# Quarter 0 of a gated projection: a written VectorE order with parts between the sums, last sums of f placed earlier, first output weights summed later

## The chip, the cores and the metric

The kernel runs on one core of one Trainium2 chip, as one launch. The metric is the device time of a launch in microseconds (us). A core has a matrix engine (TensorE, PE in the profile; its weight loads are PEld), a vector engine (VectorE, DVE), a scalar engine (ScalarE, ACT), GpSimd (POOL) and a queue that issues the transfers (SyncE, SP). Each engine takes its instructions in the order in which they stand in its queue, and waits on semaphores for what other engines produce. Matmuls write PSUM banks of 128x512 fp32; DVE, ACT and POOL read and write SBUF, and DVE and ACT read the banks.

## The reference

A graph network with four layers of cross attention and a gated feed-forward block, between two graph convolutions. N = 1024 rows, D = 512, 8 heads, 16 groups of 256 condition rows, L = 4 layers, all in fp32. What this case changes lies in the feed-forward block of each layer:

```python
for i in range(L):
    a = _attn(_ln(h, ln2_w[i], ln2_b[i]), cond, Wq[i], Wk[i], Wv[i], Wo[i])
    h = h + a
    u = _ln(h, ln3_w[i], ln3_b[i]) @ geglu_w[i] + geglu_b[i]      # (1024,512) @ (512,4096)
    val, gate = jnp.split(u, 2, axis=-1)
    f = val * jax.nn.gelu(gate, approximate=False)                 # (1024, 2048)
    h = h + f @ ffo_w[i] + ffo_b[i]                                # (1024,2048) @ (2048,512)
```

## The kernel before

**Seven products.** Large matrix products are done by a Strassen-like scheme: both operands are cut into 2x2 blocks, sums of blocks are formed (on DVE or POOL), seven block products run on PE instead of eight, and sums of the results give the output. Every product is then followed by an addition that reads its bank, and a bank is used for a second product only when that addition has read it.

**The quarters.** The feed-forward block of a layer runs in four quarters r = 0..3, each with 512 columns of val and the matching 512 of gate. Each quarter has four pieces c = 0..3 of 128 columns. A quarter gives f (tiles fT, two halves f0 and f1 per piece), and `ffn_out` multiplies f by 512 rows of the output weights and adds the result onto h.

**Quarter 0 (class `Quad`, L934 to L981).** It works in plain fp32, with four matmuls of 128x512 per product. Products 0 and 1 of each quad go to a bank ga during the end of the attention (`first`, `second`). `rest` then does products 5, 6, 4, 3, 2 into the banks gb, gc, gd, gc, gd. DVE adds: u2 from gb, u3 from gc (L967), g1 from gd (L970), g0 from gc (L974), then v1 (tile gv, L978) from gd, f1 (L980) and f0 (L981). ACT applies Gelu to g1 and g0 (L957). The fifth matmul group of a quad overwrites gd, so it waits for L970; the fourth overwrites gc after L967.

**The right blocks' parts.** The quarters 1 to 3 (class `Chunk`) use matmuls of a faster type for which every operand is split in a high, a low and a middle part. For six of the seven right blocks (ln3T and ln3S, the turned normalised rows and their sums) these parts are made once per layer, during quarter 0: `begin_right` gives the high part on ACT and the middle part gr on DVE in two halves of 128x512 (L1090), `finish_right` the low part gl, one DVE operation of 128x1024 (L1096). In `parts_beside(c)` two blocks are begun behind the last addition of each of the quads 0 to 2, and after quad 2 the low parts of blocks 0 and 1 follow. Blocks 5 and 6 get theirs ahead of the first `ffn_out`, blocks 4 and 3 ahead of the second. No order is written for this stretch: the scheduler sets each engine's order by its own estimates.

**The left parts of a chunk.** For each chunk (r, c) POOL forms sums of the weights (gxa, gy, L1138), ACT scales a high part (gha, ghb, L1103), DVE forms a low part (gla of 128x1024, glb of 128x512, L1104) and POOL their difference (gsa, gsb, L1105). The chunk's matmuls are L1154, its additions L1189 (gu, g), L1172 (a scaled addition in a bank), f0 (L1220) and f1 (L1223). These are pinned: they keep the order in which the program writes them.

**Sums of f and the output product.** `Gated.sums` (L1293 to L1301) forms the sums of f that `ffn_out` needs: for c = 0 and 1 one subtraction (a21), for c = 2 and 3 three operations fs (s2, s1, s4). `ffn_out` (L1330 to L1348) runs twice per quarter, each with seven products of eight matmuls in the order fa, fc, fd, fb, fa, fc, fd. The first fd needs fs. The first fa is read by DVE (`kept`, L1340; in quarter 0 by an ACT copy) before the second fa may overwrite its bank; fc is read by an addition onto hall (L1336) before the second fc. At a quarter boundary (r = 1 to 2, and 2 to 3) the first `ffn_out` of the old quarter stands behind the first chunk of the new one, and DVE has the old quarter's last f1, then this chunk's gu, g and glb, then the three fs, then the next chunk's gla, then `kept`.

**The output weights.** `out_weights` forms four sums on POOL (wffs, L216 to L219). For r = 0 it is written ahead of `geglu` and comes to stand, in POOL's queue, during the last attention group, whose probabilities DVE scales at L804, whose transposes DVE copies at L836 (pT), and for which PE's mixing matmuls po (L822) wait.

Of the kernel before, what the change touches and what calls it, by code (L numbers as in the profile page):

```python
# [25 lines left out]
def gnn_kernel(  # L26
# [26 lines left out]
    nc = tc.nc  # L53
# [9 lines left out]
    KC = D // P  # L63
# [19 lines left out]
    @contextmanager  # L83
    def waiting_for(ins, engine):

        traced = nc.cur_bb.bb.instructions
        n = len(traced)
        yield
        for i in traced[n:]:
            if i.engine == engine:  # L90
                tc.add_manual_dep(i, ins.ins.name, mybir.DependencyInfo(
                    mybir.DependencyClass.Sync, mybir.DependencyReason.DATA))

    def bank(name):
        return psum.tile([P, 512], F32, tag="bank", name=name)

    def t512(name, dtype=F32):
        return work.tile([P, 512], dtype, tag="t512", name=name)

    def slot(name):  # L100
        return slots.tile([P, 2, 512], F32, tag="slot", name=name)

    def slots_of(n, name):
        return [slot(f"{name}_{i}") for i in range(n)]
# [91 lines left out]
    gcols = const.tile([P, L * 2 * DFF // P], F32, name="gcols")  # L196
# [11 lines left out]
    h = [hall[:, nb, :] for nb in range(NB)]  # L208
# [4 lines left out]
    def sums_of_b(t, b11, b12, b21, b22, t1, t2, t4, t_last=None):  # L213


        t.tensor_tensor(t1, b12, b11, OP.subtract)  # L216
        t.tensor_tensor(b12, b22, b12, OP.subtract)
        t.tensor_tensor(t2, b22, t1, OP.subtract)
        return (t_last or t).tensor_tensor(t4, b21, t2, OP.subtract)  # L219
# [8 lines left out]
    def halves_of(t):  # L228
        return t.rearrange("p (a b) -> p a b", a=2)
# [62 lines left out]
    def blocks_of_w(w):  # L292
        return [w[k][:, :, d * M:(d + 1) * M] for d in range(2) for k in range(2)]
# [15 lines left out]
    def of_k(w, right):  # L309
        return lambda i, to, start: multiply(  # L310
            to, w[i], right[i], [(c * P, (c + 1) * P, 0, M) for c in range(2)], start)
# [5 lines left out]
    def begin(l, g, x, of, s1, behind=None):  # L317

        t = slots_of(2, f"{x}_{l}_{g}")
        a = bank(f"pa_{x}_{l}_{g}")  # L320
        of(0, a, True)
        nc.scalar.copy(s1, a)
        of(1, a, False)
        with tc.issue_after(behind.ins) if behind else nullcontext():
            nc.scalar.copy(blocks_out(t)[0], halves_of(a))
        return t, s1
# [51 lines left out]
    high = gp.tile([ET, P], F32, name="high")  # L378
# [17 lines left out]
    pc = bank("pc")  # L396
# [201 lines left out]
    def add_left(left, rows, to, root, name):  # L598

        for d in range(NB):  # L600
            nc.sync.dma_start(left.rearrange("p a b -> p (a b)"), left_dram[d])
            pl = bank(f"left_{name}_{d}")
            for s in range(NB):
# [8 lines left out]
             for step in project_steps(nb, h0T, w_in, "in",  # L612
# [5 lines left out]
    begun = {"k0": begin(0, 0, "kT", of_k(blocks_of_w(raw_wk), conds[0, 0]), firsts[:, 0, :],  # L618
                         shifted_last)}
# [83 lines left out]
    def acc_tile(name):  # L703
        return accs.tile([P, 512], F32, tag="acc", name=name)
# [221 lines left out]
    def out_weights(t, l, r, wff):  # L926
        s = slots_of(2, f"wffs_{l}_{r}")
        b11, b12, b21, b22 = (wff[k][:, :, d * M:(d + 1) * M] for k in range(2) for d in range(2))
        t1, t2, t4 = (halves_of(s[i // 2][:, i % 2, :]) for i in range(3))
        sums_of_b(t, b11, b12, b21, b22, t1, t2, t4)  # L930
        return [b11, b21, b22, t4, t1, t2, b12]

    class Quad:
# [5 lines left out]
            self.cv = l * 2 * DFF // P + r * KC + c  # L939
            self.left, self.right = left, right  # L940

        def product(self, i, to, start):
            multiply(to, self.left[i], self.right[i],
                     [(self.c * P, (self.c + 1) * P, 0, 512)], start)

        def first(self):
            self.a = bank(f"ga_{self.n}")
# [8 lines left out]
            cg = self.cv + DFF // P  # L956
            nc.scalar.activation(pre, pre, AF.Gelu, bias=gcols[:, cg:cg + 1])  # L957

        def rest(self):
            n, c, bias = self.n, self.c, gcols[:, self.cv:self.cv + 1]  # L960
            pb, pc, pd = (bank(f"{x}_{n}") for x in ("gb", "gc", "gd"))
            self.product(5, pb, True)
            u2 = acc_tile(f"gu2_{n}")
            nc.vector.tensor_tensor(u2, pb, self.s1, OP.add)
            self.product(6, pc, True)
            u3 = acc_tile(f"gu3_{n}")
            nc.vector.tensor_tensor(u3, pc, u2, OP.add)  # L967
            self.product(4, pd, True)
            g1 = t512(f"g1_{n}")
            nc.vector.tensor_tensor(g1, pd, u3, OP.add)  # L970
            self.gate(g1, n)
            self.product(3, pc, False)
            g0 = t512(f"g0_{n}")
            nc.vector.tensor_tensor(g0, pc, u2, OP.add)  # L974
            self.gate(g0, n)
            self.product(2, pd, False)
            v1 = acc_tile(f"gv1_{n}")
            nc.vector.scalar_tensor_tensor(v1, pd, bias, u2, OP.add, OP.add)  # L978
            f0, f1 = self.f.of(c)
            nc.vector.tensor_tensor(f1, v1, g1, OP.mult)  # L980
            return lambda: nc.vector.scalar_tensor_tensor(f0, self.a, bias, g0, OP.add, OP.mult)  # L981

    def inner_left(t, x, s1, s2, s4):

# [96 lines left out]

    SPLIT = (0, 5, 6, 4, 1, 3)

    def begin_right(name, x, h, s):

        nc.scalar.mul(h.bitcast(F32R), x, INWARD / TINY)
        for k in range(2):
            more = t512(f"{name}_{k}")
            nc.scalar.mul(more, h[:, k, :], 1.0 + TINY)
            nc.vector.scalar_tensor_tensor(s.bitcast(F32R)[:, k, :], x[:, k, :], 1.0 / TINY, more,  # L1090
                                           OP.mult, OP.subtract)

    def finish_right(name, x, h, s):

        low = slot(name)
        nc.vector.scalar_tensor_tensor(low.bitcast(F32R), x, 1.0 / TINY, h, OP.mult, OP.subtract)  # L1096
        return h, low, s

    pin = tc.keep_in_program_order

    def split_left(x, h, l, s):

# [122 lines left out]
    class KeyPair(InStep):  # L1225
# [3 lines left out]
        x = "k"  # L1229
# [77 lines left out]
    def quads_of(l, r, left, right):  # L1307
        f = Gated(l, r)
        return f, [Quad(l, r, c, left, right, f) for c in range(KC)]

    def geglu(quads, f, beside):
        for c, q in enumerate(quads):
            q.last = q.rest()()
            beside(c)
            f.sums(c)

    def ffn_out(l, r, s, left, right, kept, each=lambda ins: ins):

# [82 lines left out]
    class QueryPair(InStep):  # L1401


        x = "q"
# [134 lines left out]
    for l in range(L):  # L1539

        wk, wv, wq, wo, ffb, spare = projections
        if l:
# [13 lines left out]
            kT_1, _ = keys(l, 1, wk)  # L1556
# [169 lines left out]
        g = NG - 1  # L1726
        kT, v = kTs[g], vs[g]
        f, quads = quads_of(l, 0, left, right)
# [25 lines left out]
        raw_out = load_out(l, 0)  # L1754
        more = [slot(f"gr_{l}_{i}") for i in range(2 * len(SPLIT) - 2)]
        wide = four_wide(f"gr_{l}")
        more.extend(wide[:, 2 * i:2 * i + 2, :] for i in range(2))
        begun = {i: (right[i], *more[2 * n:2 * n + 2]) for n, i in enumerate(SPLIT)}
        Chunk.rights = {2: right[2]}

        def finish_rights(*of):
            for i in of:
                Chunk.rights[i] = finish_right(f"gl_{l}_{i}", *begun[i])

        def parts_beside(c):
            with tc.issue_after(quads[c].last.ins):
                for i in SPLIT[2 * c:2 * c + 2]:
                    begin_right(f"gt_{l}_{i}", *begun[i])
                if c == 2:
                    finish_rights(0, 1)  # L1770

        wff = out_weights(nc.gpsimd, l, 0, raw_out)
        geglu(quads, f, parts_beside)
        chunks = [(r, c) for r in range(1, R) for c in range(KC)]
        ready = []

# [11 lines left out]

        load()
        sum_chunk(0)  # L1790
        finish_rights(5, 6)
        ffn_out(l, 0, 0, f.left(), wff, kept, pin)
        split(0, False)
        split(0, True)
        load()
        sum_chunk(1)
        finish_rights(4, 3)
        ffn_out(l, 0, 1, f.left(), wff, kept, pin)
        split(1, False)
        load()  # L1800
        raw_out = load_out(l, 1)
# [5 lines left out]
        before = None  # L1807
        for r in range(1, R):
            for c in range(KC):
                chunk = ready.pop(0)  # L1810
                flow = chunk.steps(lambda: sum_chunk(1), lambda: split(0, True))
                chunk.f = f if c else Gated(l, r)
                next(flow)
                if c > 2 or r == 1 and c or r > 1 and c == 0:
                    split_next(0)
                for _ in range(3):
                    if before:
                        next(before, None)
                    next(flow)
                if before:  # L1820
                    f.sums((c - 1) % KC, nc.vector, pin)
                before = flow
                if c == 0:
                    kept_f, f = f, chunk.f
                if r > 1 and c < 2:
                    split_next(1)
                    ffn_out(l, r - 1, c, kept_f.left(), wff, kept, pin)
                    if c == 1:
                        raw_out = load_out(l, r)
                if c == (KC - 1 if r + 1 < R else KC - 2):  # L1830
                    wff = out_weights(nc.gpsimd, l, r, raw_out)
# [61 lines left out]
    class Rows:  # L1893
# [12 lines left out]
        def add(self, row, at, of, engine=nc.vector):  # L1906
            at = self.base[row][:, at]
            engine.tensor_tensor(at, of, at, OP.add)  # L1908
# [85 lines left out]
```

## Time and profile before

| what | value |
|---|---|
| time, median of 3 runs | 2483.92 us (2483.9 to 2483.96) |
| the profiled execution's own time | 2488.66 us |
| its span, first to last instruction | 2486.1 us |
| mean granted TensorE clock | 0.990 |
| busy PE, DVE, POOL, ACT | 97%, 68%, 41%, 34% |

In the profile, a row of a timeline gives start and duration in us, engine, source line, operation, output tile and input tiles, shape, count, and in brackets the idle time of the engine before it with what ended it. A row with x4 or x8 is a run of equal instructions. Rows of waits give the waiting tile and line, what it waited for, the total, the number of times and the longest. Matmuls are pipelined, so rows of PE overlap a little: the distance from start to start is the cost. A duration on DVE or POOL counts from when the instruction enters the engine, so it holds time in which it could not yet work.

### The profile page before, as it was taken

The numbers are of one execution on the slowest core, as the hardware profiler recorded it, in microseconds if no ns is written. First come the engines' busy times: TensorE is split into PE (matmuls) and PEld (weight loads), VectorE is DVE, ScalarE is ACT, GpSimd is POOL, SyncE is SP. The second block draws the span as 40 slices with busy tenths as digits, with TensorE's granted clock in tenths as the row PEclk, the third lists the DMA queues.
The fourth block names the chain that finished last, engine by engine and source line by source line (L and its number), as shares of the span: only waits on it lengthen the run. The fifth ranks groups of instructions, "written<-read, shape, count | busy, mean of one in ns | idle before, by whom it ended". The sixth has DMA issues, their size and how long they took to land. (4 is left out here: it accounts for less than half of the span.)

```text
span 2486.1 us, 35090 instructions
## 1 busy us (share of the span) xinstructions
PE 2407.7 (97%) x13032; PEld 1888.3 (76%) x13032; DVE 1696.2 (68%) x3248; ACT 839.6 (34%) x1784; POOL 1012.4 (41%) x1059
## 2 busy tenths in 40 slices
PE   8999999999999999999999999999999999999999
PEld 5678886577787887477787888477787888567787
DVE  9665566877676557776676557777785656777764
ACT  7323333343213334342313324433323333433320
POOL 0433444274453223264453224345544222536531
PEclk9999999999999999999999999999999999999999
DMA  5323220111302220011122211011131031011140
GB/s 178 121 69 113 90 94 18 42 43 51 119 31 77 89 74 18 21 56 43 56 110 68 77 66 47 9 51 51 43 132 68 14 124 52 1 51 35 51 144 35
DMA packets 118064, 163.55 MB, mean 66 GB/s; under 512 B 9256, under 2 KB 66928, under 8 KB 117888
## 3 DMA queue, kind: packets, MB, share of 16 engines
q1 hardware_dynamic: 115792, 155.81, 19.0%
q0 software_dynamic: 1376, 4.30, 0.5%
q8 instruction: 107, 1.75, 0.3%
q10 hardware_dynamic: 720, 1.11, 0.1%
q14 instruction: 69, 0.57, 0.1%
HBM read 138.12 MB, written 23.07 MB: 65 GB/s over the span
## 5 line engine op out<-in xcount | busy, mean ns | idle before, releaser
L1168 ACT ACTIVATE g<-g 128x512 f32<-128x512 f32 x192 | 112.1, 584 | 311.5 <-PE g L1154 307.7
L1105 POOL TENSOR_TENSOR gsa<-gha,gla 128x1024 fp32r<-128x1024 f32 x48 | 115.4, 2404 | 155.0 <-DVE gla L1104 155.0
L1105 POOL TENSOR_TENSOR gsb<-ghb,glb 128x512 fp32r<-128x512 f32 x48 | 79.9, 1664 | 215.4 <-DVE glb L1104 215.4
L799 ACT ACTIVATE pr<-sc,nmax 128x256 f32<-128x256 f32 x256 | 118.2, 472 | 91.6 <-DVE nmax L794 91.1
L1154 PE MATMUL g<-gr,gsa 128*128 128x512 f32 x384 | 136.6, 437 | 0.0
L1330 PE MATMUL fa<-wff,fT 128*128 128x256 f32 x512 | 124.4, 385 | 0.2
L300 PE MATMUL pa_v<-wv,ct 128*128 128x256 f32 x512 | 123.9, 385 | 0.0
L997 POOL TENSOR_TENSOR kr<-ct,ct 128x256 f32<-128x256 f32 x48 | 36.9, 768 | 211.5 <-DVE pr L804 206.9
L1154 PE MATMUL g<-gr,gha 128*128 128x512 f32 x384 | 122.8, 401 | 0.0
L300 PE MATMUL pd_v<-wvs,ct 128*128 128x256 f32 x512 | 121.0, 379 | 0.0
L300 PE MATMUL pc_v<-wv,ct 128*128 128x256 f32 x512 | 121.0, 379 | 0.0
L1154 PE MATMUL g<-gl,gla 128*128 128x512 f32 x384 | 118.6, 390 | 0.0
L1330 PEld LDWEIGHTS fa<-wff,fT 128*128 128x128 f32 x512 | 99.6, 195 | 21.3 <-issue 5.0
L300 PEld LDWEIGHTS pa_v<-wv,ct 128*128 128x128 f32 x512 | 94.9, 190 | 22.5 <-issue 9.2
L794 DVE TENSOR_REDUCE nmax<-sc 128x2 f32<-128x512 f32 x128 | 83.7, 679 | 41.2 <-PE sc L787 41.2
L1181 ACT ACTIVATE g<-g,gcols 128x512 f32<-128x512 f32 x96 | 67.4, 702 | 128.2 <-DVE g L1189 125.0
L300 PEld LDWEIGHTS pd_v<-wvs,ct 128*128 128x128 f32 x512 | 97.3, 190 | 13.2
L300 PEld LDWEIGHTS pc_v<-wv,ct 128*128 128x128 f32 x512 | 97.0, 190 | 13.0
L1330 PE MATMUL fd<-wffs,fs 128*128 128x256 f32 x256 | 71.9, 418 | 34.1 <-DVE fs L1300 34.1
L1154 PEld LDWEIGHTS g<-gr,gsa 128*128 128x128 f32 x384 | 71.9, 188 | 33.4 <-issue 16.3
L804 DVE TENSOR_SCALAR pr<-pr,inv 128x256 f32<-128x256 f32 x256 | 90.4, 396 | 2.9
L1220 DVE SCALAR_TENSOR_TENSOR fT<-g,gcols,g 128x512 f32<-128x512 f32 x48 | 35.9, 749 | 80.1 <-ACT g L1181 79.8
(516 smaller groups left out, 6352.5 us busy)
## 6 DMA issues: line engine op xcount, KB each, us to landing
ct<-cond_dram SPq DMA_DIRECT2D x72, 512.0 KB, 5.6
wff<-in_L_gnn_ffo_w_dram SPq DMA_DIRECT2D x32, 512.0 KB, 4.3
cond_dram<-ct SPq DMA_DIRECT2D x24, 512.0 KB, 3.0
gxb<-in_L_gnn_geglu_w_dram SPq DMA_DIRECT2D x96, 128.0 KB, 2.3
gxa<-in_L_gnn_geglu_w_dram SPq DMA_DIRECT2D x96, 128.0 KB, 2.3
cond<-in_L_gnn_cond_dram SPq DMA_DIRECT2D x32, 256.0 KB, 4.6
ct<-cond_dram SPq DMA_DIRECT2D x24, 256.0 KB, 5.8
wk<-in_L_gnn_Wk_dram SPq DMA_DIRECT2D x8, 512.0 KB, 6.3
```

The lines of the kernel that those rows point to most:

```text
L300: each(nc.tensor.matmul(at, left[:, k, l0:l1], right[:, k, r0:r1], start=start and n == 0 and k == 0, stop=n == len(cols_of) - 1 and k == ...
L794: nc.vector.tensor_reduce(nmax, ps3, AX.X, OP.max, negate=True)
L799: nc.scalar.activation(pr3[:, a, :], ps3[:, a, :], AF.Exp, bias=nmax[:, a:a + 1], accum_out=tot[:, a:a + 1])
L804: scores.last = nc.vector.tensor_scalar(pr3[:, a, :], pr3[:, a, :], inv[:, a:a + 1], None, OP.mult)
L997: t.tensor_tensor(to, of, less, OP.subtract)
L1105: pin(nc.gpsimd.tensor_tensor(s.bitcast(F32R), h, l, OP.subtract))
L1154: pin(nc.tensor.matmul(to, self.part(i, which)[:, k, :], self.rights[i][which].bitcast(F32R)[:, k, :], start=start and k == 0, stop=stop a ...
L1168: pin(nc.scalar.mul(to, to, 1.0 + TINY))
L1181: pin(nc.scalar.activation(to, of, AF.Gelu, bias=gcols[:, cg:cg + 1]))
L1220: pin(nc.vector.scalar_tensor_tensor(f0, a, bias, g0, OP.add, OP.mult))
L1330: each(nc.tensor.matmul(to[:, q * M:(q + 1) * M], left[i][k][:, (2 * s + q) * P:(2 * s + q + 1) * P], right[i][:, k, :], start=start and q ...
```

## The change

Each layer is changed in the same way, in five parts.

1. `Quad.rest` is pinned, on PE and DVE. After u2, u3, g1, g0 and after the end of a quad it calls `fill()`, which issues the next right block's part. v1 is replaced by an addition of u2 onto gd in the bank, f0 comes ahead of f1, and f1 reads the bank.
2. The parts come from a generator, in the order of blocks 0, 1, 5, 6, 4, 3. `finish_right` makes the low part in two halves of 128x512 instead of one operation of 128x1024, and blocks 0 and 1 get theirs right after their middle part.
3. `out_weights` for r = 0 is written after quad 0, and its POOL operations wait for the last addition of quad 0 (`q.last`).
4. In quarter 0 the sums of f of c = 0, 1 and 2 are formed on POOL instead of DVE, those of c = 3 on DVE, pinned.
5. At the boundaries from quarter 1 to 2 and 2 to 3, `f.sums(KC - 1)` of the old quarter is issued right behind its f1, two steps of the new chunk earlier than before.

On DVE the order of quarter 0 becomes, per quad: u2, part, u3, part, g1, part, g0, part, gd += u2, f0, f1, part. The sixteen parts so placed are twelve halves gr and four halves gl (blocks 0 and 1); they are used up in quad 3. Then come the three fs of c = 3, gl of blocks 5 and 6 in halves, and the additions of `ffn_out`. gl of blocks 4 and 3 are four halves behind the gla and glb of chunk (1, 0). PE's order is the same but for gb of the later quads, which is no longer split. SP's order is the same.

```diff
-        def rest(self):
-            n, c, bias = self.n, self.c, gcols[:, self.cv:self.cv + 1]
...
+        def rest(self, fill):
...
+            def add(to, x, y):
+                self.last = pin(nc.vector.tensor_tensor(to, x, y, OP.add))
+
+            self.product(5, b, True, pin)
+            add(u2, b, self.s1)
+            fill()
+            self.product(6, c, True, pin)
+            add(u3, c, u2)
+            fill()
+            self.product(4, d, True, pin)
+            add(g1, d, u3)
             self.gate(g1, n)
+            fill()
+            self.product(3, c, False, pin)
+            add(g0, c, u2)
             self.gate(g0, n)
-            self.product(2, pd, False)
-            v1 = acc_tile(f"gv1_{n}")
-            nc.vector.scalar_tensor_tensor(v1, pd, bias, u2, OP.add, OP.add)
-            f0, f1 = self.f.of(c)
-            nc.vector.tensor_tensor(f1, v1, g1, OP.mult)
-            return lambda: nc.vector.scalar_tensor_tensor(f0, self.a, bias, g0, OP.add, OP.mult)
+            fill()
+            self.product(2, d, False, pin)
+            add(d, d, u2)
+            pin(nc.vector.scalar_tensor_tensor(f0, self.a, bias, g0, OP.add, OP.mult))
+            pin(nc.vector.scalar_tensor_tensor(f1, d, bias, g1, OP.add, OP.mult))
+            fill()
...
-    def finish_right(name, x, h, s):
+    def finish_right(name, x, h):
         low = slot(name)
-        nc.vector.scalar_tensor_tensor(low.bitcast(F32R), x, 1.0 / TINY, h, OP.mult, OP.subtract)
-        return h, low, s
+        for k in range(2):
+            yield low
+            pin(nc.vector.scalar_tensor_tensor(low.bitcast(F32R)[:, k, :], x[:, k, :], 1.0 / TINY,
+                                               h[:, k, :], OP.mult, OP.subtract))
...
-        wff = out_weights(nc.gpsimd, l, 0, raw_out)
-        geglu(quads, f, parts_beside)
+        def all_parts():
+            for i in (0, 1, 5, 6, 4, 3):
+                yield from begin_right(f"gt_{l}_{i}", *begun[i])
+                if i < 2:
+                    yield from finish_rights(i)
+
+        parts = all_parts()
+        next(parts)
+
+        def fill():
+            next(parts, None)
+
+        for c, q in enumerate(quads):
+            q.rest(fill)
+            if c == 0:
+                with waiting_for(q.last, mybir.EngineType.Pool):
+                    wff = out_weights(nc.gpsimd, l, 0, raw_out)
+            f.sums(c, nc.gpsimd if c < 3 else nc.vector, pin)
+        for _ in parts:
+            pass
...
-                for _ in range(3):
+                for step in range(3):
                     if before:
                         next(before, None)
+                        if step == 2 and c == 0:
+                            f.sums(KC - 1, nc.vector, pin)
                     next(flow)
-                if before:
-                    f.sums((c - 1) % KC, nc.vector, pin)
+                if c:
+                    f.sums(c - 1, nc.vector, pin)
                 before = flow
```

More of the change, by code (lines that the diff above doesn't have):

```diff
@@ L940, in __init__, with product @@
             self.left, self.right = left, right
-        def product(self, i, to, start):
+        def product(self, i, to, start, each=lambda ins: ins):
             multiply(to, self.left[i], self.right[i],
-                     [(self.c * P, (self.c + 1) * P, 0, 512)], start)
+                     [(self.c * P, (self.c + 1) * P, 0, 512)], start, each)
         def first(self):
@@ L957, in gate @@
             nc.scalar.activation(pre, pre, AF.Gelu, bias=gcols[:, cg:cg + 1])
-        def rest(self):
-            n, c, bias = self.n, self.c, gcols[:, self.cv:self.cv + 1]
[L961 to L970, printed above, removed]
+        def rest(self, fill):
+            n, bias = self.n, gcols[:, self.cv:self.cv + 1]
+            b, c, d = (bank(f"{x}_{n}") for x in ("gb", "gc", "gd"))
+            u2, u3 = (acc_tile(f"g{x}_{n}") for x in ("u2", "u3"))
+            g0, g1 = (t512(f"{x}_{n}") for x in ("g0", "g1"))
+            f0, f1 = self.f.of(self.c)
+            def add(to, x, y):
[8 more added lines that the diff above has]
+            add(g1, d, u3)
             self.gate(g1, n)
-            self.product(3, pc, False)
-            g0 = t512(f"g0_{n}")
-            nc.vector.tensor_tensor(g0, pc, u2, OP.add)
+            fill()
+            self.product(3, c, False, pin)
+            add(g0, c, u2)
             self.gate(g0, n)
-            self.product(2, pd, False)
-            v1 = acc_tile(f"gv1_{n}")
-            nc.vector.scalar_tensor_tensor(v1, pd, bias, u2, OP.add, OP.add)
-            f0, f1 = self.f.of(c)
-            nc.vector.tensor_tensor(f1, v1, g1, OP.mult)
-            return lambda: nc.vector.scalar_tensor_tensor(f0, self.a, bias, g0, OP.add, OP.mult)
+            fill()
[4 more added lines that the diff above has]
+            fill()
     def inner_left(t, x, s1, s2, s4):
@@ L1082, in gnn_kernel @@
     SPLIT = (0, 5, 6, 4, 1, 3)
+    pin = tc.keep_in_program_order
     def begin_right(name, x, h, s):
@@ L1089, in begin_right @@
             nc.scalar.mul(more, h[:, k, :], 1.0 + TINY)
-            nc.vector.scalar_tensor_tensor(s.bitcast(F32R)[:, k, :], x[:, k, :], 1.0 / TINY, more,
-                                           OP.mult, OP.subtract)
-    def finish_right(name, x, h, s):
+            yield
+            pin(nc.vector.scalar_tensor_tensor(s.bitcast(F32R)[:, k, :], x[:, k, :], 1.0 / TINY,
+                                               more, OP.mult, OP.subtract))
+    def finish_right(name, x, h):
         low = slot(name)
-        nc.vector.scalar_tensor_tensor(low.bitcast(F32R), x, 1.0 / TINY, h, OP.mult, OP.subtract)
-        return h, low, s
-    pin = tc.keep_in_program_order
+        for k in range(2):
+            yield low
+            pin(nc.vector.scalar_tensor_tensor(low.bitcast(F32R)[:, k, :], x[:, k, :], 1.0 / TINY,
+                                               h[:, k, :], OP.mult, OP.subtract))
     def split_left(x, h, l, s):
@@ L1309, in quads_of @@
         return f, [Quad(l, r, c, left, right, f) for c in range(KC)]
[L1311 to L1315, printed above, removed]
     def ffn_out(l, r, s, left, right, kept, each=lambda ins: ins):
@@ L1762, in finish_rights @@
             for i in of:
[L1763 to L1770, printed above, removed]
-        wff = out_weights(nc.gpsimd, l, 0, raw_out)
-        geglu(quads, f, parts_beside)
+                x, high, mid = begun[i]
+                flow = finish_right(f"gl_{l}_{i}", x, high)
+                Chunk.rights[i] = high, next(flow), mid
+                yield
+                for _ in flow:
+                    yield
+        def all_parts():
[15 more added lines that the diff above has]
+            pass
         chunks = [(r, c) for r in range(1, R) for c in range(KC)]
@@ L1790, in gnn_kernel @@
         sum_chunk(0)
-        finish_rights(5, 6)
+        for _ in finish_rights(5, 6):
+            pass
         ffn_out(l, 0, 0, f.left(), wff, kept, pin)
@@ L1796, in gnn_kernel @@
         sum_chunk(1)
-        finish_rights(4, 3)
+        for _ in finish_rights(4, 3):
+            pass
         ffn_out(l, 0, 1, f.left(), wff, kept, pin)
```

## The prediction

> **What bounds the kernel now.** I read the page first, then the waits of the matmul engine, then the timelines around each of those waits.
>
> ```profile
> PE 2407.7 (97%) x13032; PEld 1888.3 (76%) x13032; DVE 1696.2 (68%) x3248; ACT 839.6 (34%) x1784; POOL 1012.4 (41%) x1059
> ```
>
> TensorE (PE) is busy for 97% of the span, and the diff takes no matmul away. So the change is worth what it does to PE's waits and to its clock. The waits of PE, grouped (total us, times, longest):
>
> ```profile
> PE fd L1330 <- DVE fs L1300: 34.1, 15, 3.6
> PE gd L300 <- DVE g L970: 18.2, 4, 5.0
> PE po L822 <- DVE pT L836: 5.8, 4, 1.5
> ```
>
> All three lie in stages that the change touches: quarter 0 (gd, and some of the fd waits), the quarter boundaries (the other fd waits), and the last attention group ahead of quarter 0 (po).
>
> **Quarter 0 as it is.** PE's timeline at the end of quarter 0, in layer 0 and (last two lines) in layer 3, then VectorE's (DVE) in layer 0, and the granted clock there (0.80, the last column but two):
>
> ```profile
> 458.85 1.88 PE L300 MATMUL gc<-ln3S,wgate 128*128 128x512 f32 x4
> 465.68 3.78 PE L300 MATMUL gd<-ln3T,ges 128*128 128x512 f32 x4 [4.95 <-DVE g L970]
> 469.25 3.07 PE L1330 MATMUL fa<-wff,fT 128*128 128x256 f32 x8
> 476.44 1.89 PE L1330 MATMUL fb<-wffs,fs 128*128 128x256 f32 x8
> ```
>
> ```profile
> 2188.78 1.88 PE L300 MATMUL gc<-ln3S,wgate 128*128 128x512 f32 x4
> 2205.61 1.89 PE L1330 MATMUL fb<-wffs,fs 128*128 128x256 f32 x8
> ```
>
> ```profile
> 458.08 1.82 DVE L1090 SCALAR_TENSOR_TENSOR gr<-ln3T,gt 128x512 fp32r<-128x512 f32 x2
> 459.82 2.34 DVE L1090 SCALAR_TENSOR_TENSOR gr<-ln3S,gt 128x512 fp32r<-128x512 f32 x2
> 462.08 2.35 DVE L1096 SCALAR_TENSOR_TENSOR gl<-ln3T,gr 128x1024 fp32r<-128x1024 f32 x2
> 464.95 0.68 DVE L970 TENSOR_TENSOR g<-gd,gu 128x512 f32<-128x512 f32 x1
> ```
>
> ```profile
> 460.00:477.00 17.00, 11.49 (x33) 7.36 (x32) 14.48 (x19) 3.50 (x5) 1.53 (x2) 0.80 0.16 46
> ```
>
> A product starts 1.72 to 1.73 us after the one before it when nothing waits (fa and fc of the boundary fence below, 555.11 and 556.84). From the start of gc to that of fb lie five products, 8.6 us; here it is 17.59, so 8.97 are lost. In layer 3 it is 16.83 (8.2 lost); between them layers 1 and 2 lose 8.45 and 7.86: 33.5 us in all. The cause is DVE's queue: it runs six right-block parts (gr, gl) before g, for whose read of bank gd the next product waits. Of the loss in layer 0 some 5.1 is that gap, 0.56 a wait of fd on fs, and 3.3 the half clock that follows (gd and fa take 3.78 and 3.07 instead of 1.88); over the four layers this tail averages 2.6 (33.5 less the waits, over 4).
>
> **Quarter 0, changed.** With g1 and g0 each ahead of a part, no more than one part stands between two sums. Per quad DVE has seven sums (0.6 each back to back) and four parts. Prices of the parts and of POOL's adds:
>
> ```profile
> 439.86 1.29 DVE L1090 SCALAR_TENSOR_TENSOR gr<-ln3T,gt 128x512 fp32r<-128x512 f32 x2
> 428.26 9.87 POOL L1611 TENSOR_TENSOR hall<-hall,ffb 128x512 f32<-128x512 f32 x8
> ```
>
> That is 7 x 0.6 + 4 x 0.65 = 6.8 us in a quad of 8.6, so DVE fits if it runs alone. It doesn't: four wffs sums, two a21 subtracts and three fs sums now sit on POOL beside it, 9 x 1.23 = 11.1 us, after the hall adds, which quad 0 already meets. Rows below show that a DVE operation with two SBUF inputs and a POOL add run one after the other. Where POOL has a queue, a part then takes about 1.3 instead of 0.65, and a quad of DVE 7 x 0.6 + 4 x 1.3 = 9.4 us, 0.8 more than PE's 8.6. The lag is small in quad 0, shows in quad 1 and is largest in quad 2, until a21 is done; quad 3 meets only fs. Laid out in queue order with these durations, PE waits 0.7 and 0.1 in quad 1, 1.8 in quad 2 and 0.1 in quad 3, 2.7 per layer (0 if POOL never collides; 5.5, twice that, if each part waits for a whole add). None is near the gaps that draw the half clock, so that tail goes, and fd hardly waits for fs: its second sum ends some 0.5 us ahead of fd, so each further 0.5 of lag in quad 3 would come back as that wait. What is late next is gl_4 and gl_3, cut into four halves behind the next chunk's splits:
>
> ```profile
> 485.88 5.58 DVE L1096 SCALAR_TENSOR_TENSOR gl<-ln3S,gr 128x1024 fp32r<-128x1024 f32 x2
> 485.44 2.73 POOL L1105 TENSOR_TENSOR gsa<-gha,gla 128x1024 fp32r<-128x1024 f32 x1 [23.84 <-DVE gla L1104]
> ```
>
> Two wide operations let two POOL operations in (5.58 us); four halves let in four, at about 7.3 us. The add on fc behind them holds PE's second fc, about 1.4 us more per layer. So layer 0 gains 8.97 - 2.7 - 1.4 = 4.9, the others 4.4, 3.8 and 4.1: **-17 us** (-28 without collisions, -6 with 5.5 us of them in each layer).
>
> The rest of quarter 0 costs nothing: the removed gv is replaced by an in-place add of the same length, f1 now reads a bank (0.66 instead of 0.60, covered by the 1.8 us a quad that DVE has spare), ScalarE's copies follow its gates at 34% busy, and no DMA is added or passes another on SP's queue. POOL's queue takes the wffs sums behind quad 0's last add; behind them wait a21, fs and the gxa sums of the next chunk, whose first reader (gsa) stands at 485, over 20 us later. Without that cover it would be 5 us.
>
> **First output weights moved: the po wait.** Timelines of layer 0 before quarter 0:
>
> ```profile
> 402.37 2.18 DVE L804 TENSOR_SCALAR pr<-pr,inv 128x256 f32<-128x256 f32 x2
> 407.28 0.62 DVE L804 TENSOR_SCALAR pr<-pr,inv 128x256 f32<-128x256 f32 x2
> 401.79 1.27 POOL L216 TENSOR_TENSOR wffs<-wff 128x512 f32<-128x512 f32 x1
> 412.94 2.08 PE L822 MATMUL po<-pT,v 128*64 128x64 f32 x62 [1.46 <-DVE pT L836]
> ```
>
> While POOL sums wffs (four such rows, to 407), a pair of scalings takes 2.18 instead of 0.62, and the next pair likewise. That delay, over 1.5 us, stands in DVE's queue ahead of the copies of the transposes for which po waits. With POOL empty there, the 1.46 goes in each layer: **-5.8 us** (0 if another link of that chain is as late).
>
> **Last sums of f at the boundaries.** Where quarter 1 meets 2 and 2 meets 3 (eight places) PE's ffn_out waits for fs. First and last of the eight (first fa, fd, second fa, fc; then first and second fa), then DVE, POOL and ACT:
>
> ```profile
> 542.88 1.89 PE L1330 MATMUL fa<-wff,fT 128*128 128x256 f32 x8
> 550.49 2.93 PE L1330 MATMUL fd<-wffs,fs 128*128 128x256 f32 x6 [3.57 <-DVE fs L1300]
> 555.11 1.89 PE L1330 MATMUL fa<-wff,fT 128*128 128x256 f32 x8
> 556.84 1.89 PE L1330 MATMUL fc<-wffs,fT 128*128 128x256 f32 x8
> ```
>
> ```profile
> 2341.63 1.89 PE L1330 MATMUL fa<-wff,fT 128*128 128x256 f32 x8
> 2353.90 1.89 PE L1330 MATMUL fa<-wff,fT 128*128 128x256 f32 x8
> ```
>
> ```profile
> 543.08 0.74 DVE L1223 SCALAR_TENSOR_TENSOR fT<-g,gcols,g 128x512 f32<-128x512 f32 x1
> 548.10 1.21 DVE L1299 TENSOR_TENSOR fs<-fT,fT 128x512 f32<-128x512 f32 x1
> 549.34 1.10 DVE L1300 TENSOR_TENSOR fs<-fs,fT 128x512 f32<-128x512 f32 x1
> 552.03 1.21 DVE L1104 SCALAR_TENSOR_TENSOR gla<-gha,gxa 128x1024 fp32r<-128x1024 f32 x1
> 553.16 0.68 DVE L1340 TENSOR_TENSOR kept<-fa,kept 128x512 f32<-128x512 f32 x1
> ```
>
> ```profile
> 543.77 2.37 POOL L1105 TENSOR_TENSOR gsa<-gha,gla 128x1024 fp32r<-128x1024 f32 x1
> 546.90 1.85 POOL L1138 TENSOR_TENSOR gxa<-gxa 128x256 f32<-128x256 f32 x2
> 549.85 1.71 POOL L1105 TENSOR_TENSOR gsb<-ghb,glb 128x512 fp32r<-128x512 f32 x1
> ```
>
> ```profile
> 545.71 0.72 ACT L1181 ACTIVATE g<-g,gcols 128x512 f32<-128x512 f32 x1 [4.80 <-DVE g L1189]
> 546.34 0.61 ACT L1103 ACTIVATE ghb<-gxb 128x512 fp32r<-128x512 f32 x1
> 548.79 1.06 ACT L1103 ACTIVATE gha<-gxa 128x1024 fp32r<-128x1024 f32 x1 [1.84 <-POOL gxa L1138]
> ```
>
> Second fa starts 12.23 us after the first (four products are 6.9): 5.33 lost; 5.37 at the last, 43.0 over the eight. Of each, 3.7 is the gap and on average 1.65 the half clock after it. The rows also show the alternation: fs from 548.10 gets going when gxa ends at 548.75; the next fs, 549.34, ends at 550.44, and gsb, recorded from 549.85, ends 1.12 later at 551.56.
>
> Changed, fs stands right behind f1, ready at 543.85. But gsa has begun at 543.77, so the first sum starts at 546.14; then DVE and POOL take turns (0.56 each): the second sum ends at 547.8, the third at 549.0. PE's fd starts near 547.9, 2.6 earlier, its wait down to 1.0. Queued behind fs are now gu, g, glb: g1 ends at 550.8 instead of 545.6. ACT's gate (0.72, then ghb 0.61, then gha 1.06) ends gha at 553.25; glb at 552.2 lets gsb in at 552.85 for 1.12, gla follows at 553.95 for 1.13, and only then kept, to 555.7. Second fa needs kept, for it overwrites the bank that kept reads. It starts at 555.75, 0.6 later than now: fb ends near 550.9, so a gap of 4.85 opens one product later. The half clock's tail then comes after it, not inside: 1.65 by the eight gaps of 3.6, 2.6 by quarter 0's four of 4.4 to 5; I take 2.1, between these. Per boundary: 5.97 + 2.1 - 5.38 = 2.7, **+21.6 us** over eight. Low end +8: the first sum beats gsa (0.55 less), gla beats gsb (0.65 less), tail 1.65. High end +31: tail 3.3, the largest of quarter 0.
>
> **The sum.** -17 - 5.8 + 21.6 = -1.2 us. The profiled execution took 2488.66 us (span 2486.1), 0.2% over the median 2483.92; the sum is laid on the median: 2482.7, say 2483. About 0.2%, 5 us, is what a measurement of this kernel tells from no change.
>
> **The rivals.**
> Kept in time (gain): at the boundaries the low end holds, so second fa loses no more than now plus a little: -22.8 + 8 = -15, 2469 us. For it: f1 and gsa are 0.08 apart, so the order of first arrival could turn. Against: the chain gate, gha, gla, kept is 5 us long whoever wins first.
> Half clock rare (gain): the tail follows only a gap that empties a whole period of 3.41 us; a gap of 4.85 does so in (4.85 - 3.41)/3.41 = 42% of positions, so the tail is 1.1: 5.97 + 1.1 - 5.38 = 1.7, +13.5, sum -9, 2475 us. Against: fd at 2.93 after a wait of 3.57, which can hardly empty one. The Trainium skill, "TensorE: Matmul & The Clock Gate" (Part 1, What's actually happening), gives this rule: half speed after at least one idle window of about 3.4 us on a free-running grid; by it the time would be 2475, and the tails after gaps of 3.57 here speak against it.
> All removed (gain): fs early ends the boundary loss and kept is never late: -43 - 22.8, 2418 us. Against: the queue order above.
> Longer half clock (slower): the gap of 4.85 leaves two periods in a row mostly idle and each boundary pays 3.3 of tail: +31 - 22.8 = +8, 2492 us. It decides from a tail of 2.9 on (+5). For it: layer 0's quarter 0 pays that after 4.95.
> Quarter 0 collides (slower): POOL adds fall on parts in a row and PE waits 5.5 instead of 2.7, -6 instead of -17: +10, 2494 us. For it: the DVE rows 458.08 and 459.82, 1.82 and 2.34 instead of 1.29 beside three small POOL adds. Against: three of four quads have DVE time to spare.
>
> **How the numbers follow.** Forecast (within 0.2%) 0.30; kept in time 0.18, half clock rare 0.12, all removed 0.05: faster 0.35. Longer half clock 0.20, quarter 0 collides 0.15: slower 0.35. Likeliest single case: 2483, by itself 2479 to 2489. The range holds all but "all removed" and the far end of both slower cases at once (2484 + 9 + 11 = 2504): 2462 to 2502.
>
> **What would show it.** PE's gd waits (18.2) nearly gone and replaced by waits below 2 us in quads 1 to 3; po waits gone; at the boundaries a wait of fd on fs near 1 us and a new wait of second fa on kept (L1340's twin) near 4.8, with fa or fc at half clock behind it; fs recorded long, beside gsa. Wrong if kept comes before 554, or if quarter 0 shows gaps above 3 us again.

## The result, and the profile after

The changed kernel takes 2477.41 us (median of 7 runs, 2476.35 to 2477.92) against 2483.98 us (median of 7 runs). The ratio is 0.9965, 95% interval 0.9954 to 0.9977: faster by 0.35%, some 6.6 us by the medians. The forecast was 2483 us, no change; the range of 2462 to 2502 holds the result, and it belongs to the 0.35 that stood on faster. The runs of the kernel before lie in two groups, near 2484 and near 2488; its profiled execution is one of the upper group, so the two profiles differ by more than the medians, 10.5 us in span.

The page of the changed kernel and its grouped waits of TensorE (total us, times, longest):

```profile
span 2475.6 us, 35108 instructions
PE 2401.2 (97%) x13032; PEld 1883.8 (76%) x13032; DVE 1701.2 (69%) x3252; ACT 837.2 (34%) x1784; POOL 1050.7 (42%) x1079
```

```profile
PE fa L1333 <- DVE kept L1343: 37.8, 8, 4.7
PE fd L1333 <- DVE fs L1309: 8.7, 11, 0.9
PE fc L1333 <- DVE hall L1339: 4.7, 4, 1.2
...
PE gc L300 <- DVE gu L967: 3.2, 4, 0.8
```

The waits of gd (18.2) and po (5.8) are gone. Of the 34.1 us of fd on fs 8.7 are left, but in their place stands a new row, second fa on kept: 37.8 us in eight places, one per boundary.

The same instruction in both timelines tells where the time went. In layer 0, the kernel before (first ga after po, first matmul of chunk (1, 0), first matmul after the first boundary's output product):

```profile
414.95 1.12 PE L300 MATMUL ga<-ln3T,wval 128*128 128x512 f32 x2
...
495.49 0.81 PE L1154 MATMUL g<-gr,gha 128*128 128x512 f32 x2
...
560.10 0.81 PE L1154 MATMUL g<-gr,gha 128*128 128x512 f32 x2
```

and the changed kernel:

```profile
412.89 1.12 PE L300 MATMUL ga<-ln3T,wval 128*128 128x512 f32 x2
...
486.92 0.82 PE L1163 MATMUL g<-gr,gha 128*128 128x512 f32 x2
...
555.10 0.81 PE L1163 MATMUL g<-gr,gha 128*128 128x512 f32 x2
```

Ahead of the changed stages the two are 0.28 apart. The lead is 2.06 after po, 8.57 after quarter 0, and only 5.00 after the first boundary. The same subtraction at these places in every layer:

| stage | forecast, us | layer 0, 1, 2, 3 | sum, us |
|---|---|---|---|
| po | -5.8 | -1.8, -1.8, -1.8, -1.8 | -7.1 |
| quarter 0 with its two output products | -17 | -6.5, -6.0, -5.4, -5.7 | -23.6 |
| two boundaries each | +21.6 | +5.4, +3.7, +7.0, +4.4 | +20.5 |

Two thirds of what the first two rows gain is given back at the boundaries.

**Quarter 0 after.** PE, DVE and POOL rows of layer 0:

```profile
449.27 1.98 PE L300 MATMUL gc<-ln3S,wgate 128*128 128x512 f32 x4 [0.80 <-DVE gu L967]
...
483.55 1.99 PE L1333 MATMUL fc<-wffs,fT 128*128 128x256 f32 x8 [1.18 <-DVE hall L1339]
```

```profile
432.96 0.69 DVE L967 TENSOR_TENSOR g<-gc,gu 128x512 f32<-128x512 f32 x1 [0.35 <-PE gc L300]
...
437.20 0.68 DVE L967 TENSOR_TENSOR gu<-gb,gs 128x512 f32<-128x512 f32 x1
...
439.49 1.15 DVE L1107 SCALAR_TENSOR_TENSOR gl<-ln3T,gr 128x512 fp32r<-128x512 f32 x1
440.56 0.68 DVE L967 TENSOR_TENSOR g<-gd,gu 128x512 f32<-128x512 f32 x1
...
446.84 0.68 DVE L967 TENSOR_TENSOR gu<-gb,gs 128x512 f32<-128x512 f32 x1
...
476.12 6.77 DVE L1107 SCALAR_TENSOR_TENSOR gl<-ln3S,gr 128x512 fp32r<-128x512 f32 x4
```

```profile
438.38 1.71 POOL L216 TENSOR_TENSOR wffs<-wff 128x512 f32<-128x512 f32 x1
...
443.53 1.61 POOL L219 TENSOR_TENSOR wffs<-wff,wffs 128x512 f32<-128x512 f32 x1
445.10 2.96 POOL L1302 TENSOR_TENSOR fT<-fT 128x512 f32<-128x512 f32 x2
```

The four wffs sums come 1.72 apart (438.38 to 443.53, three steps), with one part between each two. A part beside them costs 1.07 from start to start (439.49 to 440.56) where alone it costs 0.65, so DVE lags: quad 1 takes it 9.64 us from u2 to the next u2 (437.20 to 446.84), where PE needs 8.6 a quad. PE shows it in quad 2, 0.80 before gc. Start to start 0.96 is lost there, 0.1 more in the product behind it, and 0.1 each in quads 1 and 3: 1.25 in the layer, the same in all four. The four halves gl_4 and gl_3 take 6.77 us beside gsa, gsb and gxa, and the addition behind them holds second fc for 1.18; start to start 1.44 is lost there, against 0.24 in the kernel before.

**A boundary after.** Layer 0's first; the rows answer to those of 542 to 557 shown for the kernel before, by engine, and the last one is a stretch (length, busy time of PE, PEld, DVE, ACT and POOL, then the granted clock, 0.50):

```profile
534.34 1.89 PE L1333 MATMUL fa<-wff,fT 128*128 128x256 f32 x8
...
539.32 1.56 PE L1333 MATMUL fd<-wffs,fs 128*128 128x256 f32 x6 [0.94 <-DVE fs L1309]
540.72 1.89 PE L1333 MATMUL fb<-wffs,fs 128*128 128x256 f32 x8
547.34 3.78 PE L1333 MATMUL fa<-wff,fT 128*128 128x256 f32 x8 [4.72 <-DVE kept L1343]
550.91 2.81 PE L1333 MATMUL fc<-wffs,fT 128*128 128x256 f32 x8
```

```profile
534.55 0.74 DVE L1232 SCALAR_TENSOR_TENSOR fT<-g,gcols,g 128x512 f32<-128x512 f32 x1
535.32 2.82 DVE L1308 TENSOR_TENSOR fs<-fT,fT 128x512 f32<-128x512 f32 x1
538.17 1.10 DVE L1309 TENSOR_TENSOR fs<-fs,fT 128x512 f32<-128x512 f32 x1
539.19 1.21 DVE L1310 TENSOR_TENSOR fs<-fT,fs 128x512 f32<-128x512 f32 x1
...
543.57 0.69 DVE L1113 SCALAR_TENSOR_TENSOR glb<-ghb,gxb 128x512 fp32r<-128x512 f32 x1 [0.76 <-ACT ghb L1112]
544.51 2.17 DVE L1113 SCALAR_TENSOR_TENSOR gla<-gha,gxa 128x1024 fp32r<-128x1024 f32 x1 [0.25 <-ACT gha L1112]
546.60 0.68 DVE L1343 TENSOR_TENSOR kept<-fa,kept 128x512 f32<-128x512 f32 x1
```

```profile
535.24 2.35 POOL L1114 TENSOR_TENSOR gsa<-gha,gla 128x1024 fp32r<-128x1024 f32 x1
537.55 1.17 POOL L1147 TENSOR_TENSOR gxa<-gxa,gxb 128x256 f32<-128x256 f32 x1
...
544.34 1.26 POOL L1114 TENSOR_TENSOR gsb<-ghb,glb 128x512 fp32r<-128x512 f32 x1 [2.55 <-DVE glb L1113]
```

```profile
549.00:551.00 2.00, 2.00 (x6) 1.55 (x6) 0.27 (x1) 0.00 (x0) 1.92 (x4) 0.50 0.00 0
```

The first fs enters at 535.32, 0.08 after gsa, and stands for gsa's whole run; the next two take turns with gxa. The wait of fd falls from 3.57 to 0.94. But second fa now waits 4.72 for kept, behind fs, the chunk's sums, glb, gsb and gla, and it and fc run at half clock (3.78 and 2.81 instead of 1.89). Second fa starts 13.0 us after the first, 12.23 before the change.

### The profile page after: what moved, and what is told of

Same layout as the page of the kernel before. It is cut to its first block, busy times and chain, and to the rows that moved or that the text cites. A ratio compares the mean times of both kernels' runs of the same rounds, so it can differ in the third digit from the quotient of the medians.

```text
span 2475.6 us, 35108 instructions
## 1 busy us (share of the span) xinstructions
PE 2401.2 (97%) x13032; PEld 1883.8 (76%) x13032; DVE 1701.2 (69%) x3252; ACT 837.2 (34%) x1784; POOL 1050.7 (42%) x1079
## 5 line engine op out<-in xcount | busy, mean ns | idle before, releaser
L1114 POOL TENSOR_TENSOR gsb<-ghb,glb 128x512 fp32r<-128x512 f32 x48 | 74.2, 1545 | 240.6 <-DVE glb L1113 240.6
L1333 PE MATMUL fa<-wff,fT 128*128 128x256 f32 x512 | 135.2, 410 | 37.8 <-DVE kept L1343 37.8
L1333 PEld LDWEIGHTS fa<-wff,fT 128*128 128x128 f32 x512 | 105.1, 207 | 61.1 <-DVE kept L1343 41.0
L1113 DVE SCALAR_TENSOR_TENSOR gla<-gha,gxa 128x1024 fp32r<-128x1024 f32 x48 | 85.6, 1784 | 18.0 <-ACT gha L1112 18.0
L1226 PE MATMUL g<-ln3T,gy 128*128 128x512 f32 x192 | 90.4, 592 | 0.0
```

The costliest lines, as they stand in the source:

```text
L1113: pin(nc.vector.scalar_tensor_tensor(l.bitcast(F32R), h, -1.0 / TINY, x, OP.mult, OP.add))
L1114: pin(nc.gpsimd.tensor_tensor(s.bitcast(F32R), h, l, OP.subtract))
L1226: pin(nc.tensor.matmul(d, self.last[:, k, :], self.rights[2][:, k, :], start=False, stop=k == 1, skip_group_check=True))
L1333: each(nc.tensor.matmul(to[:, q * M:(q + 1) * M], left[i][k][:, (2 * s + q) * P:(2 * s + q + 1) * P], right[i][:, k, :], start=start and q ...
```

## The experiments

The theory: quarter 0 and po gain about 27 us by the medians, and early fs costs some 20, because kept stands behind what fs delays. The rivals: early fs is itself a gain; quarter 0's gain comes from another part than the order. Each experiment was measured beside the kernel before on its own chip, and the changed kernel was not measured again there. So a distance from the changed kernel's 2477.4 may span two chips; the ratio to the kernel before, 0.9965 for the changed kernel, is the check on it.

**The boundary part undone.**

```diff
-                        if step == 2 and c == 0:
-                            f.sums(KC - 1, nc.vector, pin)
...
-                if c:
-                    f.sums(c - 1, nc.vector, pin)
+                if before:
+                    f.sums((c - 1) % KC, nc.vector, pin)
```

> The changed kernel with one part undone: at the boundaries fs of the last piece stands behind glb again. Theory (quarter 0 and po gain, the boundaries give two thirds of it back by a wait of the second fa on kept): the boundaries lose 5.4 each again instead of 8, so 8 x 2.5 = 20 less than the changed kernel's 2477.4: 2457 us, between 2452 and 2463, with a wait of fd on fs of 3.57 in eight places and none of fa on kept. Rival (early fs is a gain and quarter 0 gave little): 2480 or more.

Measured: 2461.5 us (2460.46 to 2462.61), 16 us under the changed kernel, ratio to the kernel before 0.9888 (0.9871 to 0.9904). Its waits of fd:

```profile
PE fd L1333 <- DVE fs L1309: 29.8, 11, 3.6
```

The long wait of fd is back, no row of fa on kept is left, and the whole is faster. The rival falls: early fs is a loss. It is 2461.5 and not 2457 because all eight gaps of 3.57 now draw half clock (6.5 or 5.4 lost at each; in the profile before, two drew none and lost 4.2).

**The boundary part alone**, on the kernel before (the same lines the other way round).

> The kernel before with the boundary part alone: fs of the last piece right behind f1. Theory: eight boundaries dearer by 2.5 each, 2484 + 20 = 2504 us (2498 to 2509), waits of fa on kept near 4.7 in eight places. Rival (the boundary part is the one that gains): 2478 or less.

Measured: 2508.91 us (2508.53 to 2511.88), ratio to the kernel before on the same chip 1.0083 (1.0066 to 1.0100). Its waits:

```profile
PE fa L1330 <- DVE kept L1340: 38.1, 8, 5.0
```

Alone it makes the kernel slower by 20 us, with the wait that the theory names. So the change is a gain of 1.1% and a loss of 0.8%, measured apart.

**kept and two additions ahead of glb**, on the changed kernel. `ffn_out` became a generator that stops after the second addition onto hall; for the first output product at a boundary that much is issued ahead of `split(0, True)`, which makes glb. PE's order is the same.

```diff
+                began = []
+                def low(r=r, c=c, began=began):
+                    if r > 1 and c == 0:
+                        began.append(ffn_steps(l, r - 1, 0, f.left(), wff, kept, pin))
+                        next(began[0])
+                    split(0, True)
-                flow = chunk.steps(lambda: sum_chunk(1), lambda: split(0, True))
+                flow = chunk.steps(lambda: sum_chunk(1), low)
...
```

> The changed kernel, and at the boundaries kept and the first two additions onto hall stand ahead of glb on DVE (PE's order is the same). Theory: kept is done at 543.4 in layer 0's terms instead of 547.3, second fa waits 1.0 instead of 4.7, no half clock follows: 3.8 and about 2.1 of tail less at each of eight boundaries, 2477.4 - 47 = 2430 us (2425 to 2440). Rival (glb and gla, 2 us later, then hold the next chunk's matmuls, and the gap only moves again): 2455 to 2477.

Measured: 2431.75 us (2431.37 to 2432.79), ratio 0.9768 (0.9752 to 0.9785). PE and DVE at the first boundary of layer 0:

```profile
543.97 1.99 PE L1333 MATMUL fa<-wff,fT 128*128 128x256 f32 x8 [0.83 <-DVE kept L1343]
```

```profile
543.24 0.68 DVE L1343 TENSOR_TENSOR kept<-fa,kept 128x512 f32<-128x512 f32 x1
...
545.22 0.68 DVE L1113 SCALAR_TENSOR_TENSOR glb<-ghb,gxb 128x512 fp32r<-128x512 f32 x1
545.82 1.22 DVE L1113 SCALAR_TENSOR_TENSOR gla<-gha,gxa 128x1024 fp32r<-128x1024 f32 x1
```

Second fa waits 0.83 instead of 4.72 and runs at full clock; glb comes 1.1 us later than in the changed kernel and gla ends no later; nothing waits for them. Early fs is worth having once kept does not pay for it.

**kept alone ahead of glb** (the generator stops one line earlier, before the additions onto hall).

> The changed kernel with kept alone ahead of glb at the boundaries; the additions onto hall stay behind gla. Theory: second fa waits 1.0, but the addition that reads fc ends near 547.3, so second fc waits about 2.1; neither gap is near those that draw the half clock: 8 x (3.8 - 2.1 + 2.1 of tail) = 30 less, 2447 us (2440 to 2460). Rival (the half clock comes after two gaps of 1 and 2 us too): 2460 to 2470.

Measured: 2452.46 us (2451.09 to 2453.01), ratio 0.9851 (0.9835 to 0.9868). The gap moves as expected, to second fc. At six of the eight boundaries 4.5 are lost; at two, one in layer 0 and one in layer 3, half clock follows and 6.2 are lost. PE at that of layer 0, and stretches around it (length, then busy time of PE, PEld, DVE, ACT, POOL, then the granted clock):

```profile
614.91 2.41 PE L1333 MATMUL fc<-wffs,fT 128*128 128x256 f32 x8 [1.99 <-DVE hall L1339]
617.12 3.17 PE L1333 MATMUL fd<-wff,fs 128*128 128x256 f32 x8
```

```profile
612.90:616.30 3.40, 1.41 (x8) 1.26 (x8) 3.30 (x5) 0.00 (x0) 2.18 (x2) 1.00 0.02 5
...
617.00:619.50 2.50, 2.50 (x7) 1.96 (x7) 0.69 (x1) 0.00 (x0) 2.34 (x4) 0.50 0.00 0
```

So the rival was partly right: an idle time of 2 us can draw it.

**The first output weights back in their place**, ahead of quarter 0.

```diff
+        wff = out_weights(nc.gpsimd, l, 0, raw_out)
         for c, q in enumerate(quads):
             q.rest(fill)
-            if c == 0:
-                with waiting_for(q.last, mybir.EngineType.Pool):
-                    wff = out_weights(nc.gpsimd, l, 0, raw_out)
```

> The changed kernel with the first output weights summed where they were, ahead of quarter 0. Theory (POOL's sums hold up DVE's scalings ahead of po, and in the new place they hold up the parts of quads 1 and 2): the po wait of about 1.5 comes back in four layers with its restart, +1.8 each as the two traces differ there, and the waits of gc in quarter 0 (1.07 a layer) go: 2477.4 + 7.1 - 4.3 = 2480 us (2477 to 2483). Rival (the waits of gc come from the parts themselves and not from POOL): 2484 or more. Rival (po no longer depends on POOL): 2473.

Measured: 2482.98 us (2482.13 to 2484.15), ratio 0.9986 (0.9978 to 0.9995). Against the changed kernel's trace po costs 1.8 more in each layer, and quarter 0 0.96 less in each:

```profile
PE po L822 <- DVE pT L836: 5.9, 4, 1.5
```

No wait of gc is left among the waits. Both halves of the theory hold: POOL's sums cause the po wait in the one place and the waits of gc in the other. These make +3.3 (7.2 - 3.9). In the two traces, which are 5.7 us apart, the rest lies in the half clock after the boundaries' gaps (+2.7), which differs from trace to trace.

**gl of blocks 4 and 3 as two wide operations again.**

```diff
-        for _ in finish_rights(4, 3):
-            pass
+        for i in (4, 3):
+            block, high, mid = begun[i]
+            lower = slot(f"gl_{l}_{i}")
+            pin(nc.vector.scalar_tensor_tensor(lower.bitcast(F32R), block, 1.0 / TINY, high,
+                                               OP.mult, OP.subtract))
+            Chunk.rights[i] = high, lower, mid
```

> The changed kernel with gl of blocks 4 and 3 as two operations of 128x1024 again. Theory (DVE and POOL take turns by whole operations, so four halves let in four POOL operations and two wide ones two): the wait of second fc falls from 1.64 lost to the 0.5 of the kernel before, 2477.4 - 4.5 = 473 above 2000, 2473 us (2471 to 2475). Rival (the delay goes by bytes, not by operations): 2477.

Measured: 2473.93 us (2473.34 to 2474.25), ratio 0.9949 (0.9936 to 0.9961). The row of fc on hall is gone from the waits; start to start 0.24 is lost at that place instead of 1.44, 1.2 a layer (the expectation's 1.64 and 0.5 count some 0.2 to 0.3 too much, their difference is right). The two ratios' intervals overlap, so the gain rests on the traces, where it is the same in all four layers. Turns go by operations: the same bytes in half as many pieces let half as many POOL operations in, and gl takes 5.58 us instead of 6.77.

**a21 and the fs of quad 2 on DVE.**

```diff
-            f.sums(c, nc.gpsimd if c < 3 else nc.vector, pin)
+            f.sums(c, nc.vector, pin)
```

> The changed kernel with a21 and the fs of quad 2 on DVE instead of POOL. Theory: five operations of 0.6 more on DVE in each layer, and five POOL adds fewer that hold up a part; quad 2 with a21 has 7 x 0.6 + 0.6 + parts and stays near PE's 8.6, so within 1 us a layer of the changed kernel: 2477 us (2473 to 2481). Rival (DVE fits only because these sums went to POOL): 2485 or more, with waits of gd or gc above 2 us.

Measured: 2490.43 us (2489.25 to 2493.21), ratio to the kernel before 1.0017 (1.0008 to 1.0026). The expectation fails, the rival holds, though no wait reaches 2 us. PE and DVE in layer 0:

```profile
440.61 1.98 PE L300 MATMUL gc<-ln3S,wgate 128*128 128x512 f32 x4 [1.49 <-DVE gu L967]
...
460.60 1.98 PE L300 MATMUL gc<-ln3S,wgate 128*128 128x512 f32 x4 [1.79 <-DVE gu L967]
```

```profile
436.53 1.76 DVE L1302 TENSOR_TENSOR fT<-fT 128x512 f32<-128x512 f32 x1
...
456.74 0.68 DVE L1308 TENSOR_TENSOR fs<-fT,fT 128x512 f32<-128x512 f32 x1
457.45 0.69 DVE L1309 TENSOR_TENSOR fs<-fs,fT 128x512 f32<-128x512 f32 x1
458.06 0.68 DVE L1310 TENSOR_TENSOR fs<-fT,fs 128x512 f32<-128x512 f32 x1
```

I had counted DVE's time over a whole quad, where there is room. But the sums stand in one block ahead of u2 and u3 of the next quad: a21 meets one of POOL's last hall adds (1.76), the three fs take 1.9 in a row, and gc waits for u3. 4.6 us are lost per layer instead of 1.25. The POOL placement is a part of the gain that the diff's small line hides: 3.3 us of the 6.5 in layer 0. That the rest of it comes from the order of sums and parts is read from the rows (the 4.95 on L970 is gone); no run undoes the order alone.

**Two additions ahead of gl as well.** The kernel with kept ahead, with quarter 0's second output product begun in the same way before the low parts of blocks 4 and 3.

```diff
+        rest_out = ffn_steps(l, 0, 1, f.left(), wff, kept, pin)
+        next(rest_out)
         for _ in finish_rights(4, 3):
             pass
-        ffn_out(l, 0, 1, f.left(), wff, kept, pin)
+        for _ in rest_out:
+            pass
```

> The kernel with kept and the first two hall additions ahead of glb at the boundaries, and in quarter 0's second output product the first two hall additions ahead of the low parts gl of blocks 4 and 3 as well. Theory (second fc waits only for the addition behind gl): 1.64 less in each layer, 2431.75 - 6.5 = 2425 us (2423 to 2428). Rival (gl of blocks 4 and 3, later, hold the first chunk's matmuls): 2430 or more.

Measured: 2426.55 us (2425.62 to 2426.92), ratio 0.9758 (0.9745 to 0.9772), the fastest version of this study: 51 us under the changed kernel.

## Why the prediction was right or wrong

- *Quarter 0's waits: 2.7 a layer (bounds 0 and 5.5).* This is the step that failed in size, and it decided between no change and faster. Measured 1.25. Two terms of DVE's time per quad were off, in opposite directions. I gave a part beside POOL 1.3 us; it took 1.07 from start to start, since POOL's add and the part that follows it take 1.72 together and the sum between two parts, which reads a bank, runs while POOL adds. And I counted four parts per quad, which is the mean: five stand in each of the quads 0 to 2, one in quad 3. At 7 x 0.6 + 5 x 1.07 = 9.6 a quad of DVE beside a busy POOL does not fit into PE's 8.6, and quad 1 took 9.64; that this is near my 9.4 is luck. What I had too long is the stretch over which the lag grows. In quad 0, DVE still waits for a bank after each of the first four parts (the row of 432.96), although POOL's hall adds run beside them; and POOL's sums are done at 448.06, early in DVE's quad 2. So PE pays the lag of quad 1 alone, once, 0.96. The place (quad 2's gc) and the cause were right: with wffs elsewhere the wait went. The 1.45 too much, four times, is 5.8 us.
- *Second fc 1.4 later.* Measured 1.2 more than before (1.44 against 0.24), and two wide operations take it away. Four times, this is 0.8 us.
- *fd in quarter 0 no longer waits; no half clock there.* Right: the product fd runs in one piece at 1.9.
- *po -5.8.* Right in cause, a little small: -7.1, since the restart of the run of matmuls counts beside the wait of 1.46.
- *Boundaries +21.6.* Measured +20.5. fd's wait 1.0: 0.94. Gap at second fa 4.85: 4.72. The two together with their restarts 5.97: 6.09. Tail 2.1: the eight tails lie between 1.6 and 2.8, their mean is 1.9. kept ends at 547.28, which is 555.8 in the times of the kernel before (the first fa of the two are 8.54 apart); 555.7 was forecast. "gsa has begun before fs is ready" held by 0.08 us, and all eight boundaries show the same 6.09.
- *The sum -1.2.* Between the profiles the three rows make -10.2: 6.6 of the difference lie in quarter 0, 1.3 in po, 1.1 in the boundaries, all the same way. Laying a sum made on the profile onto the median assumed that the execution shown is like the median one. It lay 4.7 above it, so of the 11.2 us between the two profiled executions (2488.66 and 2477.45) the medians show 6.6. How much half clock follows the gaps of the kernel before differs between executions; that this is the whole of the 4.7 is argued, not shown.
- *The rivals.* "Kept in time" and "half clock rare" did not come: every one of the eight gaps has its tail. That the measured 2477 lies near the 2475 of "half clock rare" is luck, for it comes from quarter 0. The rule cited from the Trainium skill ("TensorE: Matmul & The Clock Gate", Part 1, What's actually happening), read as a window without any work, is not what these runs show: half clock followed a stretch of 3.4 us in which PE was busy for 1.41. "All removed" is not what the change does, but the experiment with kept ahead came to 2432, near its 2418. The range held the result, but the forecast of no change did not come.

## What to carry to other kernels

A sum moved forward in an engine's queue delays everything that it now stands before: follow the next reader of each delayed operation, and move with it whatever frees a bank. A change of several parts may be a gain and a loss of like size; undo each part by itself before keeping the whole. An operation that may be held up by another engine's whole operation is best placed singly, where a reader with time to spare follows, and not in a block.

## What the runs showed that I had not expected

The half clock comes on less idle time than a gap of 3.4 us: a stretch of 3.4 us with PE busy 41% of it (1.41 of 3.40, one wait of 1.99) was followed by 3.4 us at half clock, while the same wait at six other boundaries drew none. The clock records of the ten traces show why. Every stretch at half clock in them, those in the first 30 and the last 20 us of a trace aside, lasts 3.41 or 6.83 us, and within a trace all begin on one grid of 3.41 us. Laying PE's busy rows over this grid gives 6975 windows at full clock. Each of the 64 windows with PE busy for 40.5% or less was followed by half clock, and none with 44% or more; of the four between, at 41 to 42%, two were. What counts, as far as these traces show, is how much idle time falls into one window: all 40 gaps of 4.7 or 5.0 us on kept drew half clock, 14 of the 16 of 3.57 on fs in the kernel before and in the run with the boundary part undone, and 2 of the 8 of 1.99. By how the gap falls on the grid, the same wait of 3.57 thus loses between 4.2 and 6.6 us. And a DVE operation held up by POOL costs less than the whole POOL operation, 1.07 instead of 0.65 beside adds of 1.23, where the DVE operation ahead of it reads a bank.
